# Products of the identity ahead of the first transposes, two groups of transposes later, and half of the last row on ScalarE

## The chip, the cores and the metric

The kernel runs on one NeuronCore of a Trainium2 chip. The core has a matrix engine (TensorE, PE in the profile, with its weight loads listed apart as PEld), VectorE (DVE), ScalarE (ACT), GpSimd (POOL) and SyncE (SP, which here only issues DMAs). Each engine runs its own instructions in the order of the program and waits for the others on semaphores. The metric is the device time of one execution in microseconds; the median of several runs is quoted. Everything is float32.

## The reference

One transformer layer on x of 2 x 1024 x 512: causal linear attention with a residual, then a feed-forward part with 2:4 sparsity and a residual. Cut to what matters:

```python
def reference(x, Wq, Wk, Wv, Wo, w_gate, w_up, w_down):
    x = x + layernorm(attn(layernorm(x)))
    x = x + layernorm(ffn(layernorm(x)))
    return x

def attn(x):                       # 16 q heads, 4 k/v heads, head size 128
    q, k, v = x @ Wq.T, x @ Wk.T, x @ Wv.T          # split into heads
    q, k = rope(q), rope(k)
    qf, kf = elu(q) + 1, elu(k) + 1                 # k, v repeated for 4 q heads
    # over the positions s, with running sums:
    state += k_s[:, None] * v_s[None, :]
    z += k_s
    out_s = (q_s @ state) / (q_s @ z + 1e-6)
    return out @ Wo.T

def ffn(x):
    h = silu(x @ w_gate) * (x @ w_up)
    h = keep_2_largest_of_4(h)                      # by absolute value
    return h @ w_down
```

## The kernel before

**Stages.** The attention goes in 16 steps n: two passes over 8 chunks of 128 positions, each pass with half of the heads. The feed-forward part follows in 4 blocks m of 512 rows. Each projection is done as seven products in place of eight (a Strassen-Winograd scheme): `chain` (its products are numbered 1 to 7 and run in the order 1, 2, 6, 5, 7, 4, 3) multiplies sums and differences of the blocks of x by sums and differences of the blocks of the weight. `FACTORS` says which: product 1 takes blocks (weight 0, x 0), 2 takes (1, 1), 6 takes (3, 4), 5 takes (6, 3). Weight factors 3 to 6 of the first pass are summed by GpSimd (`pooled_sums`, line 604; for wq, lines 2336 and 2339, with lines 2346 and 2350 on VectorE); x factors 3 to 6 are differences by VectorE in `step_input` (lines 967 and 971).

**Start.** Two halves of x are loaded and normalized on VectorE (`step_normalize`, line 300). `step_input(0, 0)` and `step_input(0, 1)` transpose them on TensorE (`transposed`, line 651, four 128x128 transposes against an identity matrix `ident` that GpSimd writes first), ScalarE copies the results out of PSUM (lines 958 and 964), and the first products of `kv_products` and `q_products` (line 1004) begin.

**One attention step n.** The loop at the end of the main function interleaves on TensorE: products of k and v (`kvp`) and of q (`qpr`) for step n + 1, products with Wo (`opr`) for step n - 1, and for step n itself four groups i of heads: `scores(n, i)` (q by k), which VectorE masks into `am` (line 1216), then `attend(n, i)`, which multiplies `am` by v and q by the running state. `outputs(i)` is `attend(n, i)` followed by `scores(n, i + 1)`. The state is carried by VectorE (`state_sums`, lines 1234 and 1240) or copied by ScalarE in a first chunk (line 1248). `attend` also writes the products for the next state, and VectorE and ScalarE divide its result (lines 1347 to 1355).

**q before scores.** Each group of q is turned into features (`features`: VectorE lines 1030 and 1040, GpSimd 1049, ScalarE 1052 and 1054, VectorE 1057), and must then be transposed. Most groups take VectorE's 32x32 transposes and a way through DRAM (`moved`, line 879 and DMAs at lines 886 and 894). The groups in `BY_PE`, all four of step 0 and (1, 1), are transposed by TensorE in `q_transposed`, with a ScalarE copy behind (line 1129).

**PSUM.** Products and transposes use banks of three kinds: "a" (one bank, `ca`), "b" and "e" (two each, `cb` and `ce`). `scores` has one bank (`sc`) and `attend` one two-bank tile (`nm`, pool `ps_nm`). A bank is written again when its readers are done. TensorE transposes take kind "a" unless told otherwise; so does product 2 of each chain.

**Order.** The order on TensorE is the program's own, written out by hand in the main loop. The order on all other engines is computed at build time: `Plan` simulates the layer with assumed lengths (the numbers in `yield "dve", 0.45`), in up to 16 rounds, derives a latest start for every operation from the round before, and keeps the order of the round in which TensorE ends first. So a change of the program's text is followed by a new computation of the order on VectorE, ScalarE, GpSimd and SP for the whole layer. `plan.signal` and `plan.need` name the events that it orders by, and `next_part` releases pieces of the weight preparation that GpSimd does beside the first steps (line 591).

**End.** The last feed-forward block writes its rows as they come; `last_row(y, 1)` handles the last 128 rows: statistics (lines 2184 to 2192), then for each half of 256 columns a normalization (line 300) and the addition of the residual (line 2205) on VectorE and a store (line 2207) by SP for the first and by ACT's queue for the second.

Of the kernel before, what the change touches and what calls it, by code (L numbers as in the profile page):

```python
# [11 lines left out]
F32 = mybir.dt.float32  # L12
BF16 = mybir.dt.bfloat16
AF = mybir.ActivationFunctionType
ALU = mybir.AluOpType
PSUM = bass.MemoryType.PSUM

P = 128
B, S, DM = 2, 1024, 512
# [200 lines left out]
def layer(  # L220
# [17 lines left out]
    nc = tc.nc  # L238

    const = ctx.enter_context(tc.tile_pool(name="const", bufs=1))  # L240
    small = ctx.enter_context(tc.tile_pool(name="small", bufs=3))
# [4 lines left out]
    ident = const.tile([P, P], F32, name="ident")  # L246
    if not isinstance(nc, Blank):
# [8 lines left out]
        fill=0.0,  # L256
# [42 lines left out]
    def normalize(dst, src, mean, rs):  # L299
        nc.vector.tensor_scalar(dst, src, mean, rs, ALU.subtract, ALU.mult)  # L300
# [124 lines left out]
    def left(name, bufs, **more):  # L425
        return actx.enter_context(
            tc.tile_pool(name=name, bufs=bufs, reuse_waits="tile", **more)
        )
# [14 lines left out]
    ps_nm = left("ps_nm", 1, space=PSUM)  # L443
# [503 lines left out]
    def step_input(n, b, kind):  # L947

        if b == 0:
            xf[n] = ln.tile([P, 7, 2, P], F32, tag="xf", name="xf")  # L950
        t = xf[n]
        pt, name = transposed(
            xt[n][:, b, :].rearrange("p (c d) -> p c d", c=NIC), kind, ("xn", n, b)
        )

        def first():
            yield "act", 0.65, 0
            nc.scalar.copy(t[:, 0:2].rearrange("p q k d -> p (q k) d"), pt)
            plan.signal(name)
            plan.signal(("xf0", n))  # L960

        def second():
            yield "act", 0.4, 0
            nc.scalar.copy(t[:, 2], pt[:, 2:4, :])
            yield "xf0", n
            yield "dve", 0.45, 0
            nc.vector.tensor_tensor(t[:, 3], pt[:, 0:2, :], t[:, 0], ALU.subtract)
            plan.signal(name)
            for to, i0, i1 in ((4, 2, 3), (5, 4, 0), (6, 1, 4)):
                yield "dve", 0.45, 0  # L970
                nc.vector.tensor_tensor(t[:, to], t[:, i0], t[:, i1], ALU.subtract)
            plan.signal(("xf", n))
            yield "sp", 0.44, 2
            nc.sync.dma_start(out=xf_dram[n], in_=t)
            yield plan.transfer(896)
            plan.signal(("xf stored", n))

        plan.spawn((first, second)[b]())
# [590 lines left out]
    def run(g, times):  # L1569
        for _ in range(times):  # L1570
            next(g, None)
# [605 lines left out]
    def last_row(y, row):  # L2177
        m, yt = NM - 1, y[:, 2 + row, :]
        yield "y row", row, "a"
        yield "dve", 0.45, 2  # L2180
        st = layernorm_stats(yt[:, 256:512], f"l{row}")
        yield "y row", row, "b"
        yield "dve", 0.45
        nc.vector.bn_stats(st[:, 1, :], yt[:, 0:256])
        mv = small.tile([P, nc.vector.BN_AGGR_DIM], F32, tag=f"mvl{row}", name="mv")
        yield "dve", 0.2
        nc.vector.bn_aggr(mv, st)
        rs = small.tile([P, 1], F32, tag=f"rsl{row}", name="rs")
        yield "act", 0.3
        nc.scalar.activation(rs, mv[:, 1:2], AF.Sqrt, bias=eps)  # L2190
        yield "dve", 0.2
        nc.vector.reciprocal(rs, rs)
        if row == 0:
            yield from write_output(m, 2, (mv[:, 0:1], rs), "dve")
            return
        yn, _ = yield from take("ln", 4, new_yn)
        b, c = place(m, 3)
        yield "residual", m, 3
        xr, _ = res.pop((m, 3))
        for k, queue in enumerate((nc.sync, nc.scalar)):  # L2200
            half_ = slice(256 * k, 256 * k + 256)
            yield "dve", 0.3
            normalize(yn[:, half_], yt[:, half_], mv[:, 0:1], rs)
            yield "dve", 0.42
            nc.vector.tensor_tensor(yn[:, half_], xr[:, half_], yn[:, half_], ALU.add)  # L2205
            yield ("sp", "act")[k], 0.44
            queue.dma_start(out=out[b, c * P : (c + 1) * P, half_], in_=yn[:, half_])
# [119 lines left out]
    with tc.manual_schedule(engines={E.PE, E.Pool, E.SP, E.DVE, E.Activation}):  # L2327
# [51 lines left out]
        plan.spawn(step_normalize(1, None, 0))  # L2379
        plan.spawn(prepare_all())  # L2380
        plan.need(("xn", 0, 1))
        step_input(0, 0, "a")
        step_input(0, 1, "e")
        kvp, qpr = kv_products(0), q_products(0)
        run(kvp, 5)
        run(qpr, 2)
# [7 lines left out]
        for n in range(STEPS):  # L2394
            more = n + 1 < STEPS

            def next_part():
                nonlocal part
                plan.signal(("part", part))
                part += 1  # L2400

            def outputs(i, n=n):
                if n not in (NC - 2, NC):
                    next_part()
                attend(n, i)
                if i < 3:
                    scores(n, i + 1)
                elif 1 < n < STEPS - 1:
                    scores(n + 1, 0)

            if 0 < n < NC - 2:
                next_part()
            if n + 3 < NC:
                plan.spawn(load(n + 3, "x"))
            if n + 2 < STEPS:
                if n + 2 < NC:
                    plan.spawn(step_normalize(n + 2, ("root", n)))
                else:
                    plan.spawn(step_input_again(n + 2))
            if n + 2 == NC:  # L2420
                plan.spawn(load_pass(1, "wq", 2, 512, q_quarter, wq_dram, ("q", n + 1)))
                plan.spawn(load_pass(0, "wkv", 2, 256, kv_quarter, wkv_dram, ("k", n + 1)))
            elif n == NC:
                plan.spawn(load_pass(2, "wo", 4, 256, o_quarter, wo_dram, ("o", n - 1)))
            previous, opr = opr, (o_products(n - 1) if n > 0 else None)
            if n > 0:
                plan.spawn(o_sums(n - 1))
            if n > 1:
                run(previous, 2)
            if not more:  # L2430
                break
            kvp, qpr = kv_products(n + 1), q_products(n + 1)
            run(qpr, 1)
            if n == 2:
                scores(2, 0)
            if n == 0:
                run(qpr, 1)
                run(kvp, 1)
                k_transposed(0, "e")
                q_transposed(0, 0, "e")  # L2440
                run(qpr, 1)
            else:
                run(kvp, 1)
                run(qpr, 1)
                if n == 1:
                    k_transposed(1, "e")
                    first_state(1, 0)
                elif n == NC + 1:
                    first_state(n, 0)
                run(qpr, 1)  # L2450
                if n == 1:
                    scores(1, 0)
                    q_transposed(1, 1)
                    o_transposed(0, 3, "e")
            run(kvp, 1)
            plan.signal(("root", n))
            if n > 0:
                outputs(0)
            else:
                scores(0, 0)  # L2460
            if n + 2 < STEPS:
                plan.spawn(load(n + 2, "rope"))
            run(kvp, 1)
            run(qpr, 1)
            if n == 0:
                q_transposed(0, 1)
                outputs(0)
            run(kvp, 1)
            run(qpr, 1)
            run(kvp, 1)  # L2470
            if n == 0:
                q_transposed(0, 2)
                outputs(1)
                run(kvp, 1)
                run(qpr, 1)
                q_transposed(0, 3)
                run(kvp, 1)
                step_input(2, 0, "a")
                outputs(2)
                step_input(2, 1, "a")  # L2480
                run(qpr, 1)
                outputs(3)
            else:
                outputs(1)
                run(qpr, 1)
                run(kvp, 1)
                run(qpr, 1)
                run(kvp, 1)
                run(opr, 2)
                outputs(2)  # L2490
                if n + 2 < NC:
                    step_input(n + 2, 0, "a")
                run(opr, 2)
            if n + 2 == STEPS:
                plan.need(("prepared",), *(("features", n + 1, i) for i in range(4)))
                rctx.close()
                begin_ffn()
            if n > 0:
                k_transposed(n + 1)
                run(opr, 1)  # L2500
                if n + 2 < NC:
                    step_input(n + 2, 1, "a")
                outputs(3)
# [117 lines left out]
```

## Time and profile before

Three runs: 1264.67, 1262.66 and 1264.32 us, median 1264.32. One execution was profiled.

| | |
|---|---|
| profiled execution, device time | 1261.97 us |
| its span in the profile | 1260.2 us |
| PE busy | 1241.0 us (98%), 6344 instructions |
| PEld busy | 991.6 us (79%) |
| DVE busy | 921.7 us (73%) |
| ACT busy | 478.6 us (38%) |
| POOL busy | 365.7 us (29%) |
| DMA | 266.04 MB, mean 211 GB/s |

The span runs from the first to the last recorded instruction or transfer, and 1.77 us of the device time lie around it. In timelines a row gives start, length, engine, line, operation, tile written and tiles read, shapes and the number of instructions merged; a matmul's length holds its way through the pipeline, so rows overlap, and the distance between starts is the pace. What stands in brackets is the engine's idle time ahead of the row, and what ended it. In the list of waits each row has the engine, its tile and line, then what it waited for, the total, the number of times and the longest. TensorE is nearly always busy, and the idle time of the other engines costs nothing by itself.

### The profile page before, as it was taken

How to read it: one execution, taken by the hardware profiler on the slowest of the kernel's cores; microseconds unless marked ns; L12 is line 12 of the kernel's file. 1: busy time of each engine (PE TensorE's matmuls, PEld its weight loads, DVE VectorE, ACT ScalarE, POOL GpSimd, SP SyncE). 2: the span in 40 equal slices, each digit the busy share in tenths (PEclk: the TensorE clock that was granted, in tenths of full speed). 3: DMA queues.
4: the chain of work that ended last, by engine and by line, in shares of the span. 5: the costliest groups of instructions: out<-in, count | busy, mean ns of one | idle time of the engine just before them, and what ended most of it. 6: DMA issues, size and time to landing. Idle time of an engine off the chain costs nothing. (4 is left out here: it accounts for less than half of the span.)

```text
span 1260.2 us, 18691 instructions
## 1 busy us (share of the span) xinstructions
PE 1241.0 (98%) x6344; PEld 991.6 (79%) x6344; DVE 921.7 (73%) x1751; ACT 478.6 (38%) x941; POOL 365.7 (29%) x319
## 2 busy tenths in 40 slices
PE   7999999999999999999999999999999999999997
PEld 4667776777667776777688888988889988998886
DVE  6898877777656777778764489658993699656873
ACT  3664454443343354445443332133312432133311
POOL 4554443332422455455421105331010101001100
PEclk9999999999999999999999999999999999999999
DMA  7368857678758876676564796589746976677413
GB/s 268 118 223 256 270 185 242 230 229 288 235 190 245 268 231 235 230 227 199 179 193 159 198 269 185 182 237 278 221 126 203 278 214 197 192 232 223 143 50 118
DMA packets 285166, 266.04 MB, mean 211 GB/s; under 512 B 20496, under 2 KB 237072, under 8 KB 282384
## 3 DMA queue, kind: packets, MB, share of 16 engines
q1 hardware_dynamic: 283696, 262.88, 66.9%
q10 hardware_dynamic: 1376, 1.97, 0.5%
q8 instruction: 51, 0.84, 0.3%
q14 instruction: 43, 0.35, 0.1%
HBM read 189.53 MB, written 75.24 MB: 210 GB/s over the span
## 5 line engine op out<-in xcount | busy, mean ns | idle before, releaser
L685 ACT COPY u<-cb 128x512 f32<-128x512 f32 (+1 forms) x234 | 115.7, 496 | 355.3 <-PE cb L1004 117.0
L1355 ACT ACTIVATE o<-nm,den 128x128 f32<-128x128 f32 x256 | 81.5, 367 | 121.2 <-DVE den L1349 79.1
L1049 POOL TENSOR_TENSOR qraw<-qraw,r 128x512 f32<-128x512 f32 x48 | 62.8, 1308 | 214.8 <-DVE qraw L1040 179.6
L1452 PE MATMUL cb<-wo,of 128*128 128x256 f32 x512 | 123.5, 384 | 0.3 <-ACT u L685 0.2
L1004 PE MATMUL cb<-wq,xf 128*128 128x512 f32 x256 | 121.9, 599 | 0.0
L1452 PEld LDWEIGHTS cb<-wo,of 128*128 128x128 f32 x512 | 93.7, 190 | 20.8 <-issue 7.9
L591 POOL TENSOR_TENSOR wraw<-wraw 128x512 f32<-128x512 f32 x68 | 95.5, 1404 | 2.4
L2044 POOL TENSOR_TENSOR h<-h 128x512 f32<-128x512 f32 x16 | 26.8, 1683 | 235.6 <-DVE ht L2033 181.4
L381 PE MATMUL cb<-fxnT,wgu 128*128 128x256 f32 x384 | 87.6, 379 | 0.0
L381 PE MATMUL cb<-fxt,wgu 128*128 128x256 f32 x368 | 84.0, 380 | 0.0
L1004 PEld LDWEIGHTS cb<-wq,xf 128*128 128x128 f32 x256 | 47.2, 190 | 44.7 <-issue 42.8
L381 PEld LDWEIGHTS cb<-fxnT,wgu 128*128 128x128 f32 x384 | 72.7, 190 | 9.8
L381 PEld LDWEIGHTS cb<-fxt,wgu 128*128 128x128 f32 x368 | 69.5, 190 | 10.0 <-ACT u L685 0.8
L1004 PEld LDWEIGHTS cb<-wkv,xf 128*128 128x128 f32 x256 | 47.9, 192 | 31.6 <-issue 25.6
L698 DVE TENSOR_TENSOR y<-u,ce 128x256 f32<-128x256 f32 (+1 forms) x42 | 18.8, 449 | 72.4 <-ACT u L685 57.4
L1004 PE MATMUL cb<-wkv,xf 128*128 128x256 f32 x256 | 68.2, 389 | 0.0
L1452 PE MATMUL ce<-wo,of 128*128 128x256 f32 x256 | 60.5, 379 | 0.0
L2157 POOL TENSOR_TENSOR fyn<-res,fyn 128x512 f32<-128x512 f32 x12 | 15.3, 1275 | 154.8 <-issue 96.0
L1004 PE MATMUL ce<-wq,xf 128*128 128x512 f32 x128 | 60.1, 592 | 0.0
L1057 DVE SCALAR_TENSOR_TENSOR qraw<-qraw,r 128x512 f32<-128x512 f32 x48 | 42.6, 887 | 21.9 <-ACT r L1054 21.7
L2061 PE MATMUL cb<-wd,h 128*128 128x256 f32 x256 | 57.3, 379 | 0.0
L1987 ACT ACTIVATE s<-h 128x1024 f32<-128x1024 f32 x32 | 32.7, 1053 | 64.6 <-DVE h L1983 64.6
(225 smaller groups left out, 2767.2 us busy)
## 6 DMA issues: line engine op xcount, KB each, us to landing
wgu<-us SPq DMA_DIRECT2D x63, 256.0 KB, 4.3
qb<-blocks SPq DMA_DIRECT2D x59, 256.0 KB, 2.3
qT<-qb SPq DMA_DIRECT2D x236, 64.0 KB, 2.7
ob<-blocks SPq DMA_DIRECT2D x58, 256.0 KB, 3.0
of<-ob SPq DMA_DIRECT2D x232, 64.0 KB, 2.6
xf<-xf SPq DMA_DIRECT2D x16, 896.0 KB, 5.1
wd<-in_w_down_dram SPq DMA_DIRECT2D x24, 512.0 KB, 5.7
wd<-d_dram SPq DMA_DIRECT2D x24, 512.0 KB, 5.1
```

The costliest lines, as they stand in the source:

```text
L381: nc.tensor.matmul(bank[:, j, :].rearrange("p (w t) -> p w t", t=32), w[:, k, j, :], xf[xi][:, k], start=(start and j == 0 and k == 0), st ...
L591: nc.gpsimd.tensor_tensor(to, i0, i1, op)
L685: nc.scalar.copy(kept[i], b)
L698: nc.vector.tensor_tensor(dst[:, rows], kept[i][:, rows], b, ALU.add)
L1004: nc.tensor.matmul(bank.rearrange("p h d -> p (h d)"), xf[n][:, xi, k, :], w[wi][:, k, :], start=(start and k == 0), stop=(k == 1), skip_g ...
L1049: nc.gpsimd.tensor_tensor(u, u, r, ALU.add)
L1057: nc.vector.scalar_tensor_tensor(f, u, 0.0, r, ALU.max, ALU.add)
L1355: nc.scalar.activation(t[:, u, :], nmv[:, u // 2, u % 2, 0:HD], AF.Copy, scale=den[:, u // 2, u % 2 : u % 2 + 1],)
L1452: nc.tensor.matmul(bank.rearrange("p h d -> p (h d)"), of[n, xi][:, k, :], weights[gp][2][wi][:, k, :], start=(start and k == 0), stop=(k ...
L1987: nc.scalar.activation(a[:, k::2, :], h[:, k::2, :], AF.Abs)
L2044: nc.gpsimd.tensor_tensor(b12, b22, b12, ALU.subtract)
L2061: nc.tensor.matmul(b[:, j if row is None else 0, :], hts_or_h(m, jb, hi)[:, k, j * P : (j + 1) * P], w[jb][:, k, :], start=(start and part ...
```

## The change

Three things in the order on TensorE, and one in the last row:

- Before the first two `step_input` calls, 18 products of the identity with itself are issued into a new `nm` tile that nobody reads, and two more after these calls. The plan is not told of them.
- In step n = 1, `q_transposed(1, 1)` moves from before `o_transposed(0, 3)` to behind `attend(1, 0)`; one k/v product stands between it and `scores(1, 1)`, which followed `attend(1, 0)` directly before.
- In step n = 0, the two `step_input(2, ...)` calls move behind `outputs(2)` and behind the q product that follows.
- In `last_row`, the second half is normalized by ScalarE as scale * y + shift, with a shift of -mean * scale made by VectorE first; the first half and both additions stay on VectorE.

```diff
@@ last_row
         xr, _ = res.pop((m, 3))
+        shift = small.tile([P, B], F32, tag="shift", name="shift")[:, 0:1]
+        yield "dve", 0.15
+        nc.vector.scalar_tensor_tensor(shift, mv[:, 0:1], -1.0, rs, ALU.mult, ALU.mult)
+        halves = [slice(256 * k, 256 * k + 256) for k in range(2)]
+        yield "act", 0.4
+        nc.scalar.activation(
+            yn[:, halves[1]], yt[:, halves[1]], AF.Identity, bias=shift, scale=rs
+        )
+        yield "dve", 0.4
+        normalize(yn[:, halves[0]], yt[:, halves[0]], mv[:, 0:1], rs)
         for k, queue in enumerate((nc.sync, nc.scalar)):
-            half_ = slice(256 * k, 256 * k + 256)
-            yield "dve", 0.3
-            normalize(yn[:, half_], yt[:, half_], mv[:, 0:1], rs)
+            half_ = halves[k]
             yield "dve", 0.42
             nc.vector.tensor_tensor(yn[:, half_], xr[:, half_], yn[:, half_], ALU.add)
@@ main
         plan.need(("xn", 0, 1))
+        fill = ps_nm.tile([P, 2, 512], F32, tag="nm", name="fill")
+
+        def filler(count):
+            for _ in range(count):
+                nc.tensor.matmul(fill[:, 0, 0:P], ident, ident, start=True, stop=True)
+
+        filler(18)
         step_input(0, 0, "a")
         step_input(0, 1, "e")
+        filler(2)
         kvp, qpr = kv_products(0), q_products(0)
@@ main, in the loop over n
                 if n == 1:
                     scores(1, 0)
-                    q_transposed(1, 1)
                     o_transposed(0, 3, "e")
             run(kvp, 1)
             plan.signal(("root", n))
-            if n > 0:
+            if n > 1:
                 outputs(0)
+            elif n == 1:
+                next_part()
+                attend(1, 0)
+                q_transposed(1, 1)
             else:
                 scores(0, 0)
             if n + 2 < STEPS:
                 plan.spawn(load(n + 2, "rope"))
             run(kvp, 1)
+            if n == 1:
+                scores(1, 1)
             run(qpr, 1)
@@ main, n == 0
                 q_transposed(0, 3)
                 run(kvp, 1)
+                outputs(2)
                 step_input(2, 0, "a")
-                outputs(2)
+                run(qpr, 1)
                 step_input(2, 1, "a")
-                run(qpr, 1)
                 outputs(3)
```

## The prediction

> **What bounds the kernel now.** I read the busy shares first: TensorE (PE) is busy 1241.0 of 1260.2 us, so only its idle time (19.2 us) and slow stretches can be won. The waits of PE, longest first, say where the idle time is.
>
> ```profile
> engine line waited for: us in total, times, longest us
> PE ca L651 <- DVE x L300: 7.6, 1, 7.6
> PE ca L651 <- DVE qraw L1057: 1.6, 1, 1.6
> PE cb L1859 <- DMA wgi<-gs: 0.8, 1, 0.8
> PE ca L381 <- DMA wgu<-in_w_gate_dram: 0.6, 1, 0.6
> PE ca L651 <- ACT qT L1129: 0.5, 1, 0.5
> ...
> PE ca L1004 <- ACT qT L1129: 0.2, 1, 0.2
> ```
>
> The first is the wait for the first normalized x. The 1.6, 0.5 and 0.2 lie at 69.25, 53.75 and 70.55 us, in the stages that the change reorders; the 0.8 and 0.6 lie after 700 us and are not touched. The last matmul ends at about 1253.6, so the tail is another 6.6 us. Next, the timeline of PE at the start.
>
> ```profile
> 7.62 1.09 PE L651 MATMUL ca<-ident,x 128*128 128x128 f32 x4 [7.62 <-DVE x L300]
> 8.49 1.06 PE L651 MATMUL ce<-ident,x 128*128 128x128 f32 x4
> 9.38 2.08 PE L1004 MATMUL cb<-wkv,xf 128*128 128x256 f32 x4
> 11.25 1.40 PE L1004 MATMUL ca<-wkv,xf 128*128 128x256 f32 x4
> 12.48 1.03 PE L1004 MATMUL cb<-wkv,xf 128*128 128x256 f32 x4
> ...
> 25.82 0.60 PE L651 MATMUL ce<-ident,x 128*128 128x128 f32 x4
> ```
>
> Four transposes take 1.06 here and 0.60 later; four products of 256 columns are 1.87 apart (9.38 to 11.25) and later 0.86 (12.48 to 13.34). So PE works at half rate from 7.62 to about 12.0, 4.4 us, although the granted clock of that stretch reads 1.00: here only the durations show it. Last, how full the engines are by stage (columns: stretch, length, then busy time and instructions of PE, PEld, DVE, ACT, POOL).
>
> ```profile
> 55.40:67.00 11.60, 11.49 (x46) 6.10 (x44) 11.46 (x19) 7.64 (x20) 7.40 (x7) 1.00 0.82 264
> 67.00:71.50 4.50, 2.70 (x17) 1.92 (x17) 4.46 (x9) 1.66 (x3) 0.95 (x1) 1.00 0.87 292
> 71.50:80.00 8.50, 8.50 (x45) 5.66 (x44) 7.69 (x19) 4.72 (x10) 3.35 (x3) 1.00 0.72 251
> ```
>
> From 55.4 to 71.5 VectorE (DVE) is busy 15.92 of 16.1 us: there it sets the pace, and the reader should doubt that PE can simply run ahead.
>
> **Part 1, products of the identity.** Added: 18 products and, after the transposes, 2. The identity is written by 1.51 us, so they begin at about 1.6. The nearest row is a 128x128 product at full rate, 0.112 apart (four L1859 products from 800.38 to 800.83); at half rate 0.22, so 18 take 4.0 us and end near 5.6, hidden in the 7.6 us wait. They write the nm bank, whose first other use is at 41.38: nothing waits for them. If all 20 were slow, the last two cost 2 x 0.22 = 0.44 on the path.
>
> What a full rate wins, on PE alone: the ca group ends 0.60 after 7.62, at 8.22; the ScalarE (ACT) copy L958 (0.59, now 8.74 to 9.33) ends at 8.84; the first k/v product starts at 8.89 in place of 9.38; two groups of 0.86 later, at 10.61, the third (factor 6) could start, which now starts at 12.48: 1.87 us. But that product reads a weight sum from POOL and an x difference from DVE.
>
> ```profile
> 9.79 1.26 POOL L604 TENSOR_TENSOR wkv<-wkv,wkv 128x512 f32<-128x512 f32 x1
> 10.46 0.88 DVE L971 TENSOR_TENSOR xf<-xf 128x256 f32<-128x256 f32 x1
> 12.42 1.45 POOL L604 TENSOR_TENSOR wkv<-wkv,wkv 128x512 f32<-128x512 f32 x1
> 12.67 1.48 DVE L971 TENSOR_TENSOR xf<-xf 128x256 f32<-128x256 f32 x1
> ```
>
> POOL's sum ends at 11.05 whatever PE does (its own wait was for the weights' DMA), and the DVE difference, 0.42 long elsewhere (L967), ends at 11.34, 0.29 after POOL; the last one ends 14.15, 0.28 after POOL's 13.87. So each waits for POOL's, and factor 6 starts at about 11.5: 12.48 - 11.5 = 1.0. Of the 1.87, 0.9 turns into a new wait of PE. I take 1.0; the bounds are -0.4 (clock not raised) and 1.4 (POOL's 11.05 alone). What follows (q products, their sums on POOL to 18.79 for a product at 20.23) leaves 1.4 us of room, so the gain travels on.
>
> The Trainium skill, "SBUF — State Buffer", section "SBUF: two separate sides", says that a VectorE operation with two SBUF inputs and a GpSimd one that reads SBUF exclude each other for the whole instruction, and the first to start wins. The difference would now be ready at about 9.70, before POOL's 9.79; by the rule POOL's sum would then end at 11.4, and the gain would be 1.0 again.
>
> By the rows the half rate lasted 4.4 us from the first product, and the 18 products last 4.0, then PE idles about 2 us: that speaks against the filler. The Trainium skill, "TensorE: Matmul & The Clock Gate", Part 1, puts the rise at about 3.4 us of activity in a free-running window, and the fall at an idle window of the same length; by it the clock would rise between 5.0 and 8.4 us and survive the gap, and a late rise would cost up to half of the gain.
>
> **Part 2, the third step's x transposes later (n = 0).** Same instructions. Now PE has finished a product at 53.09 and stands to 53.75 (0.66) because L651 needs the ca bank, freed by the qT copy (ends 53.70); attend(0, 3) starts at 58.65 in place of 58.38 (0.27). Put behind outputs(2), the transposes find the bank free, and attend(0, 2) moves up; it needs the nm bank, freed by the state copy L1248, 53.57 to 53.87 on an ACT that is busy 2.60 of 2.60 us in 50.5 to 53.1. If ACT keeps its order, attend starts 0.3 earlier; if the x normalization (L939, 0.80, at 50.36) goes back, all 0.93 comes. I take 0.6, bounds 0.2 and 0.95. The second x transpose comes later by some 1 us, and its differences (three L971, 63.09 to 66.82) feed the q product at 65.12: a loss here goes to the second rival.
>
> **Part 3, the second step's q transposes later (n = 1).** PE's gaps between scores(1, 0) (ends 67.61) and 74.92 are 1.64, 0.41, 0.11 and 0.11, 2.27 in all. In the new order o_transposed, one k/v product (0.86) and attend(1, 0) (1.85) go ahead of q_transposed. Queued behind attend on PE is all else, and it waits for am and the state sums. Before L1057's qraw (ends 69.07) nothing on DVE changes; add mid 0.25, am 0.41, state 0.27 and kraw<-u,ca 0.41, which frees the ca bank for q_transposed: 69.07 + 1.34 = 70.41. PE reaches q_transposed at 67.61 + 0.43 + 0.86 + 1.85 = 70.75. So DVE just keeps up, with L1057 on u (0.68) and two stream transposes (0.71, 0.69) put off; the q DMAs behind the first of them (a qb store at 70.47, four reads on SP from 72.82, 2.7 to land) can slip by the 2.1 us of these three operations, since scores(1, 2), which reads them, stands at 81.93. The moved x transposes bring one DMA, the xf store (L974, at 66.88), read again only in the second pass. With parts 1 and 2 PE comes up to 1.6 earlier, of which DVE can follow the 1.0 of part 1; some 0.4 to 0.7 is lost. I take 1.6, bounds 0.5 (am stays at 70.96) and 2.2.
>
> **Part 4, the last row.** Now rs (ends 1255.41), normalize 0.41, add 0.43, normalize 0.41, add 0.42, issue at 1257.19. Removed: one DVE normalize (it spaces the next by 0.44). Added: a 128x1 shift, 0.15 with 0.05 to start it (L932), and an ACT half, about 0.45 (copies of 128x256 take 0.37, L939 of 128x512 0.80), beside DVE's half. 0.44 - 0.20 = 0.24. I take 0.2, bounds -0.8 (an ACT table load, 1.28 as at 1247.35, in the path) and 0.25. That Sqrt is followed by a scaled Copy with no load (43.48, 43.69) speaks against the load.
>
> **Sum.** 1.0 + 0.6 + 1.6 + 0.2 = 3.4 us. The profiled execution took 1261.97 (span 1260.2 and 1.77 around it), so 1258.6 for one like it; the median of the three runs, 1264.32, lies 2.35 higher, and 1264.32 - 3.4 = 1260.9.
>
> **Rivals.** The build computes the order of DVE, ACT, POOL and SP anew for the whole kernel, so every stage's order may move; the rivals live there and in the clock.
> First, the clock is not up at 7.6: part 1 gives 0 to -0.4, the rest 2.4: 1264.32 - 2.2 = 1262.1. For: 4.0 against 4.4 us. Against: the transposes add 0.9 to it.
> Second, DVE takes the gain: PE meets it at the q product at 65.12 or at attend(1, 0), and parts 2 and 3 give their lower 0.2 and 0.5, with part 1 halved: 0.2 + 0.5 + 0.5 + 0.2 = 1.4, 1262.9. For: 15.92 of 16.1. Against: DVE's work there is the same, and 0.8 us of it is free by 80.
> Third, slower: the one 0.32 wait of the ca bank for DVE's y (L698), at 135.83, in n = 2, comes back in each of the 14 steps under the new order: 14 x 0.32 = 4.5, less 3.4: 1265.4. It decides from 11 steps on. For: DVE is busy 9.37 of 10 us in 130 to 140. Against: from 140 to 400 PE waits for nothing at all.
> Fourth, the reordering has no effect since the transposes were never last: against it, the 1.6 stands on the very instruction that moves. It would give 1.2, 1263.1, and I count it with the second.
>
> **Chances.** The forecast 0.60 (own range 1259.3 to 1261.8), clock 0.13, DVE 0.15, slower order 0.12. A run of this kernel tells about 0.2% (2.5 us) from no change, so faster means below 1261.8, slower above 1266.8. Faster: 0.60 and a little of the clock rival, 0.62. Slower: the worse half of the third, 0.08. Same: 0.30. The best bounds add to 1.4 + 0.95 + 2.2 + 0.25 = 4.8, 1259.5, and 0.5 for the spread of the runs shown makes the low end 1259.0; the high end, 1264.3, takes in the clock and DVE rivals and leaves the third out.
>
> **What would show it.** Right: in the profile after, transposes of 0.60 at 7.6 and a k/v group 0.86 apart, with PE standing about 0.9 before factor 6 near 11.5; no L651 wait for qraw near 69; the q product that now starts at 74.92 at about 71.7 (74.92 less 3.2); the last issue at about 0.2 less after rs. Wrong: groups of 1.87 at the start; a new PE wait for xf (L971) or am (L1216) between 60 and 72; a table load ahead of the ACT half; waits of 0.3 in many later steps.

## The result and the profile after

The changed kernel takes 1264.41 us (median of 22 runs, 1262.19 to 1268.02), the kernel before, run beside it, 1262.56 (22 runs, 1261.44 to 1265.22, the three already known among them): a ratio of 1.0017, 95% interval [1.0009, 1.0024]. It is slower by 1.85 us where a gain of 3.4 was forecast. The profiled execution took 1262.19 us (span 1260.5), the fastest of its 22, so the traces of before and after differ by less than the medians do.

TensorE's waits in the changed kernel:

```profile
PE fill L2394 <- POOL ident masks.py:199: 1.6, 1, 1.6
PE ca L651 <- ACT kT L1111: 0.9, 1, 0.9
PE ca L651 <- DVE kraw L698: 0.9, 1, 0.9
PE cb L1859 <- DMA wgi<-gs: 0.8, 1, 0.8
PE ce L1452 <- DVE y L698: 0.7, 1, 0.7
PE cb L1452 <- ACT u L685: 0.7, 2, 0.5
PE ce L651 <- DVE kf L1057: 0.6, 1, 0.6
```

The 1.6 us wait for `qraw` is gone. In its place stand two, for `kf` at 63.5 and for `kraw` at 70.2 (0.6 and 0.9), and a third that is new, 0.9 at 98.6, behind the copy of the transposed keys. (Those for `y` and `u`, at 312 and 468 us, come and go between traces of one kernel: e8, the kernel before once more, waits 0.8 for `u`.) The start, from its timeline:

```profile
1.56 6.95 PE L2394 MATMUL fill<-ident 128*128 128x128 f32 x36 [1.56 <-POOL ident masks.py:199]
8.35 0.60 PE L651 MATMUL ca<-ident,x 128*128 128x128 f32 x4
8.79 0.60 PE L651 MATMUL ce<-ident,x 128*128 128x128 f32 x4
9.22 0.61 PE L2394 MATMUL fill<-ident 128*128 128x128 f32 x4
9.67 1.09 PE L1004 MATMUL cb<-wkv,xf 128*128 128x256 f32 x4
10.19 4.09 POOL L604 TENSOR_TENSOR wkv<-wkv,wkv 128x512 f32<-128x512 f32 x3
10.34 4.22 DVE L971 TENSOR_TENSOR xf<-xf 128x256 f32<-128x256 f32 x3
10.59 1.03 PE L1004 MATMUL ca<-wkv,xf 128*128 128x256 f32 x4
11.88 1.10 PE L1004 MATMUL cb<-wkv,xf 128*128 128x256 f32 x4 [0.26 <-DVE xf L971]
```

The clock is up: transposes of 0.60 instead of 1.09, products 0.92 apart instead of 1.87. But the 18 products of the identity are 36 records, last until 8.5 and hold the transposes back to 8.35, where they began at 7.62 before; 0.26 of that is x, whose statistics begin at 4.66 instead of 4.40. The third product of `wkv`, which the prediction put at 11.5, starts at 11.88 (12.48 before).

Engines by stretch, in the columns of the prediction's table:

```profile
55.40:67.00 11.60, 10.96 (x46) 5.68 (x44) 11.50 (x18) 7.48 (x19) 7.22 (x6) 1.00 0.92 294
67.00:71.50 4.50, 3.59 (x32) 3.13 (x31) 4.46 (x8) 1.89 (x4) 3.23 (x3) 1.00 0.68 277
71.50:80.00 8.50, 8.50 (x44) 5.49 (x44) 7.19 (x20) 6.66 (x14) 2.54 (x2) 1.00 0.56 198
```

DVE is still busy 15.96 of 16.1 us from 55.4 to 71.5; PE gained 0.89 us of work in the second stretch (2.70 to 3.59) and lost 0.53 in the first (11.49 to 10.96). The end:

```profile
1256.19 0.15 DVE L2192 RECIPROCAL rs<-rs 128x1 f32<-128x1 f32 x1
1256.38 0.16 DVE L2202 SCALAR_TENSOR_TENSOR shift<-mv,rs 128x1 f32<-128x1 f32 x1
1256.46 0.41 DVE L300 TENSOR_SCALAR fyn<-y,mv,rs 128x256 f32<-128x256 f32 x1
1256.62 0.60 ACT L2205 ACTIVATE fyn<-y,shift,rs 128x256 f32<-128x256 f32 x1 [0.58 <-DVE shift L2202]
1256.91 0.77 DVE L2213 TENSOR_TENSOR fyn<-fx,fyn 128x256 f32<-128x256 f32 x2
1257.71 0.36 ACTq L2215 DMA_DIRECT2D out_dram<-fyn  x1
```

From the end of `rs` (1256.34) to the last issue it now takes 1.37 us, 1.78 before; there is no table load.

### The profile page after: what moved, and what is told of

Its sections match the earlier page's. It is cut to its first block, busy times and chain, and to the rows that moved or that the text cites. A ratio compares the mean times of both kernels' runs of the same rounds, so it can differ in the third digit from the quotient of the medians.

```text
span 1260.5 us, 18755 instructions
## 1 busy us (share of the span) xinstructions
PE 1247.0 (99%) x6384; PEld 997.1 (79%) x6384; DVE 924.1 (73%) x1751; ACT 480.2 (38%) x942; POOL 366.0 (29%) x319
## 4 chain that ended last, share of the span: by engine, by line
PE 86%; DVE 6%; DMA 4%; ACT 1%; issue 1%; SPq 1%; POOL 0%; DVEq 0%; ACTq 0%; POOLq 0%
PE cb L381 14%; PE cb L1004 11%; PE cb L2061 9%; PE cb L1452 7%; PE ce L381 7%; PE ce L1004 5%; PE ce L2061 4%; PE ce L1452 3%; PE ca L381 3%; PE nm L1317 3%; PE cb L1859 3%; PE ca L1004 3%; PE ca L2061 2%; PE nm L1328 2%; PE sc L1203 2%; PE ca L1452 2%
```

## The experiments

Sixteen runs follow (e4, e8 and e16 are known kernels again), each with one profile and five rounds beside the kernel before. Besides the ratio I compare traces by stage: the same TensorE groups are matched in both traces, and the distance between their starts is followed. The table gives what each stage adds to the profiled execution of before (us; negative is a gain); the stages end where, in the first trace of before, these times are reached.

| kernel | to 13.3 | to 62.4 | to 74.9 | to 112 | to 986 | to 1247 | tail | ratio |
|---|---|---|---|---|---|---|---|---|
| after | -0.52 | -0.90 | -0.22 | +1.26 | +0.90 | +0.41 | -0.68 | 1.0017 |
| e4 after again | -0.02 | -0.92 | +0.18 | +1.27 | +0.10 | +1.39 | -0.68 | 1.0016 |
| e1 filler alone | +0.31 | 0 | 0 | 0 | +0.60 | +0.96 | 0 | 1.0012 |
| e7 filler of 8 | +0.55 | 0 | +1.62 | 0 | +1.75 | +0.66 | 0 | 1.0003 |
| e9 wide filler | -0.37 | 0 | 0 | 0 | +3.95 | 0 | 0 | 1.0001 |
| e2 no filler | -0.30 | -0.90 | -0.22 | +1.25 | +0.35 | 0 | -0.67 | 0.9997 |
| e13 after, wide | +0.15 | -0.90 | -0.21 | +1.26 | +2.70 | 0 | -0.66 | 1.0002 |
| e12 no filler, bank e | +1.01 | -0.91 | -0.21 | +0.40 | +0.94 | 0 | -0.67 | 0.9994 |
| e10 x later, last row | +0.57 | +0.33 | -1.25 | 0 | +3.83 | 0 | -0.75 | 0.9990 |
| e11 q later, last row | -0.33 | +0.87 | -2.06 | +1.04 | +6.21 | 0 | -0.65 | 1.0011 |
| e16 before once more | +0.65 | 0 | 0 | 0 | +3.23 | +3.88 | 0 | 1.0008 |
| e8 before again | +0.86 | 0 | +1.62 | 0 | +0.63 | 0 | 0 | 0.9989 |
| e3 old due times | +0.02 | +0.14 | +2.94 | +0.10 | +1.72 | 0 | -0.65 | 1.0023 |
| e5 qT reads first | +0.56 | -0.31 | -0.62 | +1.27 | +1.71 | 0 | -0.74 | 1.0012 |
| e6 e5, bank e | -0.02 | -0.32 | -0.83 | +1.26 | +1.52 | 0 | -0.75 | 0.9998 |
| e14 e13, bank e | -0.06 | -0.91 | -0.23 | +0.40 | +2.50 | 0 | -0.68 | 0.9996 |
| e15 e10, wide | +0.03 | +0.33 | -1.05 | 0 | +2.72 | 0 | -0.75 | 0.9990 |

The column "to 986" varies by several us between traces of one kernel (0, 0.6 and 3.2 for before), so only what repeats is used; the column "to 1247" is 0 in twelve of these rows, and what it holds in the three rows with 18 and 2 products (after, e4, e1) is the first finding. In e16 it is the delayed end of one store at 1017 us (line 300 waited 3.5 us for it) and a fall of the clock behind it; in e7 0.50 of the 0.66 lie at the same place, where line 300 waited 1.4 us for the store.

### The kernel before against itself

e8 and e16 are the kernel before; e4 is the changed kernel once more.

> The kernel before, for a second profile of it: how far the landing of wv (7.89 in the first), the wait at scores(1, 0) and the waits for gi at 988 and 1131 vary without any change. If the landing of wv and the waits at 988 and 1131 vary as much here as with filler, neither is the filler's doing.

> The kernel before against itself beside these three: a ratio within 0.0010 of 1; its runs with a mean granted clock of 0.997 some 1.5 to 1.9 us above those with 0.999, if the fall of the clock at 67 to 72 us makes them.

> The changed kernel once more, for a second profile beside the same runs of before. The 22 times of after lie in two heaps, near 1263.8 and near 1266.4. Theory A: the second heap is the filler running at half rate to its end (36 x 0.22 = 7.9 us, so first transposes near 9.5), and a profile of that heap shows it. Theory B: the start is alike in all runs, and the heaps differ in waits further on.

In e8 and e16 the first weight sum on GpSimd, which waits for Wv, starts at 8.25 and 8.43 us instead of 7.97, and neither has a wait for `gi` near 988 or 1131. The trace of e4 is of a run of 1263.26, so it shows the lower heap once more, and no trace shows the upper one. Against itself the kernel before gave 0.9989 [0.9981, 0.9998] and 1.0008 [0.9997, 1.0019]. So a difference of 0.1% can't be told here, whatever its interval says. The changed kernel's 1.0017 came again as 1.0016 [1.0005, 1.0028] and lies outside.

The profiled run of e8 took 1265.06. In it the granted clock, whose changes the trace records, fell to half at 71.84 us for 3.41 us. The same stretch in the trace of before, then in e8:

```profile
70.55 1.13 PE L1004 MATMUL ca<-wkv,xf 128*128 128x256 f32 x4 [0.24 <-ACT qT L1129]
71.52 0.61 PE L1317 MATMUL nm<-state,qT 128*128 128x129 f32 x4
71.96 0.61 PE L1317 MATMUL nm<-mid,qT 128*128 128x129 f32 x4
```

```profile
71.43 1.71 PE L1004 MATMUL ca<-wkv,xf 128*128 128x256 f32 x4 [0.24 <-ACT qT L1129]
72.93 1.06 PE L1317 MATMUL nm<-state,qT 128*128 128x129 f32 x4
73.79 1.06 PE L1317 MATMUL nm<-mid,qT 128*128 128x129 f32 x4
```

Groups that start 0.44 apart before are 0.86 apart here, and the stage costs 1.62 us. The fall follows the waits at 67 to 71 us. Windows of the clock's own grid, 3.41 us long, with TensorE's busy time in them: the one that ends at the fall in e8, and the one at the same place in the trace of before, after which the clock stayed up:

```profile
68.43:71.84 3.41, 1.60 (x12) 1.00 0.96 333
```

```profile
66.60:70.01 3.41, 1.85 (x13) 1.00 0.86 316
```

Busy for 1.60 us it fell, for 1.85 it did not; where the grid lies differs from run to run. Over the 140 runs of the kernel before that stood beside the experiments, the mean is 1263.23 us at a mean granted clock of 0.999 (87 runs), 1264.28 at 0.998 (43) and 1264.79 at 0.997 (10): up to 1.56 more, as expected. A reading of 0.998 can be a fall (e7) or none (e13), as the clock also falls when TensorE is done, at the end of every trace. The changed kernel read 0.998 in one of its 34 runs and 0.997 in none, so this is not why it is slower.

### The products of the identity

e1 is the kernel before with the 18 and 2 products alone; e2 the changed kernel without them; e7 before with 8 and none behind. The order on the other engines is exactly that of the kernel that each is made from.

```diff
 e1:  +filler(18) ... +filler(2)
 e2:  -filler(18) ... -filler(2)
 e7:  +filler(8)
```

> The kernel before with the 18 + 2 products of the identity alone; the order on every other engine is unchanged. Theory A (the filler overruns the wait it was meant to fill, since each product is two matmuls in the trace, 36 in all and 6.8 us in the profile after, and by an amount that varies): first transposes at 8.3 us or later in place of 7.6, the time between 0.6 us below and 3 us above before, with a wider spread than before. Theory B (the filler does what it should and the loss is all in the new order): 0.6 to 1.0 us below before, spread as before.

> The changed kernel without the products of the identity; its order on VectorE, ScalarE, GpSimd and SP is that of the changed kernel. Theory A: faster than the changed kernel by about what the filler alone costs, 1262 or below where before is 1262.6. Theory B: about 0.6 us slower than the profile of after, and the waits that the profile after shows at 312, 468 and 99 us (0.7, 0.5, 0.9) stand here too, so 1263.5 to 1265.

> The kernel before with 8 products of the identity (16 matmuls, 3.5 us at half rate, done by about 5.1) and none behind the transposes. If the filler costs by overrunning: as before or up to 0.6 us faster. If the start is bound by the weights' DMA and the sums on POOL (wv lands at 7.9 to 9.1, factor 6 starts 3.2 to 3.6 after it), no filler wins more than 0.6, and this one is within 0.5 of before. If the cost is in what the added TensorE instructions move later on (the instruction fetches of TensorE at 985 and 1128 us beside the gate loads): waits for gi near 988 and 1131 come or go with the place of these fetches.

e1: 1.0012 [1.0001, 1.0023]. e2: 0.9997 [0.9986, 1.0007]. e4 and e2 stood beside the same runs of before, with medians of 1265.53 and 1262.33. So the loss comes with the products, not with the moves. In the trace of e1 it is not the overrun of theory A: the transposes start at 7.70 instead of 7.62. e7: 1.0003 [0.9992, 1.0014]. Eight products did not raise the clock (full at 13.31 us; 11.98 in the trace of before); with 18 it is full at 7.19, 6.30 and 5.34 (after, e4, e1). The early clock is real, yet in e1 nothing is won by 13.3 us, and between 986 and 1247 us 0.96 is lost. What TensorE and its weight loads wait for near 988 in e4, then the landing times of the `gi` loads there, in three views of this tile (e4; e13, with the wide filler told of next; before):

```profile
PEld cb L1859 <- DMA wgi<-gi: 0.4, 1, 0.4
PE cb L1859 <- DMA wgi<-gi: 0.2, 1, 0.2
```

```profile
DMA to landing us min/median/max: 4.0/5.4/6.3
```

```profile
DMA to landing us min/median/max: 4.0/4.4/4.9
```

```profile
DMA to landing us min/median/max: 4.5/4.8/5.0
```

The longest takes 6.3 us, 1.3 more than before. The trace has DMA records of kind "instruction": on one queue 51 of 16 KB, about 1 us long, one for some 256 instructions of TensorE, which fits its code. The change adds 80 TensorE instructions (18 + 2 products, two matmuls and two weight loads each), which brings every later fetch forward in the program: from 990.95 and 1130.35 us (before) to 985.32 and 1127.50 (after), 985.22 and 1127.94 (e1), just ahead of the late products at 988 and 1131. The theory: the fetch delays the loads that TensorE is about to need. The landings of one `gi` load near 988 and of one near 1131 fit it in all 18 traces: in after, e1 and e4, where the fetch runs while they are under way, they take 5.80, 6.08 and 6.29 us, and 5.94, 6.19 and 6.42; in the other fifteen, where it does not (in e7 it begins 0.03 us before the second lands), 4.49 to 5.03 and 4.45 to 5.22. In e7, with 32 instructions more, neither wait is there. e9 and e13 fill the same time with a fifth of the instructions, in the kernel before and in the changed one:

```diff
-                nc.tensor.matmul(fill[:, 0, 0:P], ident, ident, start=True, stop=True)
+                nc.tensor.matmul(
+                    fill[:, 0, :].rearrange("p (j d) -> p j d", j=4),
+                    ident,
+                    ident.unsqueeze(1).to_broadcast([P, 4, P]),
+                    start=True, stop=True,
+                )
...
-        filler(18)
+        filler(4)
...
-        filler(2)
```

> The kernel before with 4 products of the identity with four copies of itself (128x512 each) ahead of the first transposes: about as long as the 18 narrow ones (6.1 to 6.9 us by the rows so far), but 16 instructions of TensorE instead of 72 (80 with the two behind). The other engines' order is that of the kernel before. Theory (instruction fetches): the late waits of TensorE for wgi at 988 and 1131, 0.4 to 1.4 us in all four kernels with the filler of 18 and 2 and in no other, come from the added instructions, which move the 16 KB fetch of TensorE's code, one per 256 instructions, from 969 to 985 us; with 16 they move by about 1.4 us, so the waits are gone (below 0.15 us), and the ratio to before is 0.9985 to 1.0003. Rival (the waits follow from the moved start, or from the clock's early rise): the waits stay, 0.4 us and more, and the ratio is 1.0008 to 1.0015. Both expect the full clock at 5 to 7.5 us and the start within 0.5 us of before's.

> The changed kernel with 4 wide products of the identity (16 instructions of TensorE) in place of the 18 and 2 narrow ones (80 instructions); the other engines' order is the changed kernel's. Theory: the changed kernel is slower because its filler's instructions move TensorE's code fetches onto the gate weights' loads at 985 and 1127; without that, waits for wgi at 988 and 1131 below 0.15 us each, and a ratio of 0.9990 to 1.0000 against 1.0017 of the changed kernel. Rival (the new order, or the filler's early clock, makes it slow): 1.0010 to 1.0020 as before.

e9: 1.0001 [0.9992, 1.0009]; e13: 1.0002 [0.9992, 1.0011], 0.0002 above what was expected. The clock is full at 5.19 and 6.01 us, and the loss after 986 us is gone: 0.00 in e9, e13, e14 and e15, all with the wide filler, against 0.41, 0.96 and 1.39 in the three traces with 18 and 2 narrow products. The two pairs, 1.0012 to 1.0001 and 1.0017 to 1.0002, put some 1.4 and 1.9 us on the narrow products; with a kernel straying 0.1% against itself these sizes are rough, and what they hold beyond the late waits is not located. That the added instructions make the late waits is shown; that the fetch itself holds the loads up rests on the landings above, as no run moved the fetch alone.

Why does the start win so little? e13 from 9.5 us on:

```profile
9.54 1.80 DVE L971 TENSOR_TENSOR xf<-xf 128x256 f32<-128x256 f32 x3
9.79 1.03 PE L1004 MATMUL ca<-wkv,xf 128*128 128x256 f32 x4
11.15 2.55 POOL L604 TENSOR_TENSOR wkv<-wkv,wkv 128x512 f32<-128x512 f32 x2
12.53 1.13 PE L1004 MATMUL cb<-wkv,xf 128*128 128x256 f32 x4 [1.71 <-POOL wkv L604]
```

The second product starts 1.46 earlier than before (11.25 to 9.79), and the third 0.05 later, since it waits 1.71 us for POOL's sum. VectorE's differences are ready sooner and start first, and POOL's sum begins only at 11.15, near the end of the third (11.34), and ends at 12.47, where the prediction had 11.05 "whatever PE does". In the changed kernel above it was the other way round: POOL at 10.19, then the differences from 10.34, three in 4.22 us. That agrees with the Trainium skill, "SBUF — State Buffer", "SBUF: two separate sides": one excludes the other, the first to start wins. POOL's first sum, which waits for the DMA of Wv, starts anywhere from 7.97 to 9.13 us over the traces. Over seven traces with the clock up early the third product starts at 12.31 us in the mean (11.88 to 12.69), over ten without any filler at 12.64 (12.05 to 13.03): 0.33 us gained, no more than the spread within either group.

### The two moves

e10 has only the x transposes later, e11 only the q transposes, both with the new last row and without products of the identity.

> The kernel before with the third step's x transposes later (n = 0) and the last row's half on ScalarE; no filler, no move of the second step's q transposes. Theory (the 1.25 us lost between 75 and 112 belong to the move of the q transposes): 1.0 us gained by 62, 0.6 to 0.7 at the end, nothing lost in 75 to 112: 1.6 us, ratio 0.9987, unless the clock falls at 67 to 72, which costs 1.6 us. Rival (any newly planned order gives it back there): 1.0 us gained, 0.8 or more lost in 75 to 112, ratio 0.9995 or above.

> The kernel before with the second step's q transposes later (n = 1) and the last row's half on ScalarE. Theory: 0.2 us gained in 62 to 75, 1.25 lost in 75 to 112 (TensorE waits some 0.9 for the copy of the transposed keys, L1111), 0.65 gained at the end: ratio 1.0003. Rival (the loss comes with the x transposes' order): nothing lost in 75 to 112, ratio 0.9993.

To 62.4 us, where the x transposes lie, after and e2 gain 0.90: TensorE no longer stands before them. The q move alone (e11) gains 2.06 from 62.4 to 74.9; the 0.87 that e11 loses earlier lie at 20 us, where TensorE waits for GpSimd's sums of wq, far from the move. Both moves together gain 1.12 from 13.3 to 74.9 (after and e2; 0.74 to 1.15 in eight traces with both in a newly planned order). They do not add: together they bring TensorE ahead of DVE, which is busy all the time there, and 0.8 is lost at 64.2 with the wait for `kf` and 1.0 more than in e11 at 73.4 with that for `kraw`. Alone, e11 has no wait of TensorE from 60 to 75 us at all.

The 0.92 that e10 gains by 74.9 (0.72 in e15) is not what was expected, 1.0 by 62. By 62.4 it has lost 0.33, as the second transposes wait for a ScalarE copy; then the 1.6 us wait for `qraw` is gone though its transposes did not move, since the newly computed order makes this `qraw` 6 us earlier on VectorE. One line of before, then two of e10:

```profile
68.42 0.68 DVE L1057 SCALAR_TENSOR_TENSOR qraw<-qraw,r 128x512 f32<-128x512 f32 x1
```

```profile
59.15 0.66 PE L651 MATMUL ca<-ident,x 128*128 128x128 f32 x4 [0.57 <-ACT xf L958]
62.21 0.69 DVE L1057 SCALAR_TENSOR_TENSOR qraw<-qraw,r 128x512 f32<-128x512 f32 x1 [0.77 <-ACT r L1054]
```

So a move alone, with an order computed for it, is not a part of the two together. e10: 0.9990 [0.9979, 1.0001]; e11: 1.0011 [1.0002, 1.0020]. Its theory had the loss behind the move, but 0.2 in place of the 2.06; its order loses 1.04 at 97 us, where TensorE waits 0.7 for GpSimd, and, in its profile, 3.7 between 112 and 300.

In 75 to 112 us, e10 loses nothing, and every kernel with both moves in a newly planned order loses 1.25, unless the bank is changed (e12, e14). The place is 98 us. First before, then e2:

```profile
94.02 0.26 DVE L1234 TENSOR_TENSOR mid<-nm,state 128x129 f32<-128x129 f32 x1
94.70 0.81 DVE L1057 SCALAR_TENSOR_TENSOR qraw<-qraw,r 128x512 f32<-128x512 f32 x1
95.03 2.95 POOL L591 TENSOR_TENSOR wraw<-wraw 128x512 f32<-128x512 f32 x2
98.26 0.59 ACT L1111 COPY kT<-ca 128x512 f32<-128x512 f32 x1 [1.52 <-PE ca L651]
```

```profile
94.26 3.28 POOL L591 TENSOR_TENSOR wraw<-wraw 128x512 f32<-128x512 f32 x2
94.66 1.75 DVE L1057 SCALAR_TENSOR_TENSOR qraw<-qraw,r 128x512 f32<-128x512 f32 x1
97.13 0.26 DVE L1234 TENSOR_TENSOR mid<-nm,state 128x129 f32<-128x129 f32 x1
97.42 0.62 ACT L1355 ACTIVATE o<-nm,den 128x128 f32<-128x128 f32 x2 [2.27 <-DVE mid L1234]
98.92 0.59 ACT L1111 COPY kT<-ca 128x512 f32<-128x512 f32 x1
99.56 0.66 PE L651 MATMUL ca<-ident,x 128*128 128x128 f32 x4 [0.93 <-ACT kT L1111]
```

Two things make `mid` late. The new order puts it behind the `qraw` of line 1057, which it stood ahead of; and while DVE's operation started first before, POOL is now 0.40 ahead, and it takes 1.75 instead of 0.81. No run separates the two. ACT waits 2.27 for it with the key copy behind, and TensorE waits for the bank that this copy frees. e12 and e14 give the transposes behind it another bank; e14 has the wide filler too.

```diff
-                    step_input(n + 2, 1, "a")
+                    step_input(n + 2, 1, "e" if n == 1 else "a")
```

> The changed kernel without the filler, with the second half of the fourth step's x transposes (n = 1) in a bank of kind e in place of ca. Theory (what is lost at 98 is the wait for the ca bank that the key copy still holds): the wait of 0.93 us is gone, and 0.6 to 0.9 us of the 1.25 lost in 75 to 112 come back; ratio 0.9991 against 0.9997 of the kernel without this edit. Rival (VectorE, held up by GpSimd's sum at 94.3, is late for all that follows): TensorE waits for something else by 101, the stage still loses 1.0 or more, ratio 0.9997.

> The same with the second half of the fourth step's x transposes in a bank of kind e, so that both losses found are taken away: theory 0.9985 to 0.9995 (the 0.9994 of the kernel without any filler and with this bank, less up to 0.4 us at the start); rival: no better than 0.9997.

The wait is gone, and the stage loses 0.40 instead of 1.25 in both, as the theory had it. Ratios 0.9994 [0.9985, 1.0003] and 0.9996 [0.9986, 1.0005], which can't be told from those without the edit (0.9997, 1.0002). The best found adds the wide filler to e10, with no move of the q transposes:

> The kernel before with the third step's x transposes later, the last row's half on ScalarE and the 4 wide products; the second step's q transposes stay. Theory: 0.4 us at the start, 1.05 by 75, 0.65 at the end, 2.1 us in all, ratio 0.9983 to 0.9990. Rival (the start gains nothing, since the weights' DMA and GpSimd's sums set it): 0.9990 as without the products.

0.9990 [0.9977, 1.0002], as without the filler. With e10 that is twice 0.1% below the kernel before, no more than this kernel strays against itself: neither can be called faster.

### The order on the other engines

e3 makes both moves and the new last row, but the due times by which the other engines' order is computed are taken from the text of before; it has no products of the identity. e5 is e2 with the reads of `of` for group (0, 1) held until those of `qT` for (1, 0) have been issued on SP; e6 is e5 with `q_transposed(1, 1)` in a bank of kind e.

```diff
 e5:  +        if name == ("of", 0, 1):
      +            yield "qT sent", 1, 0
 e6:  -                q_transposed(1, 1)
      +                q_transposed(1, 1, "e")
```

> The reordering of TensorE and the last row's half as in the change, without filler, but VectorE, ScalarE, GpSimd and SP keep the priorities that the build computes for the kernel before; their order differs from before only up to about step 3 and in the last row. Theory B (the loss comes from priorities computed anew in stages that the change does not touch): no waits of PE for y or u at 312 and 468 us, and 1.0 to 2.0 us below before. Rival (the moved transposes themselves cost the time): as slow as the changed kernel without filler.

> The changed kernel without filler, with one dependence more: the four reads of of(0, 1) go to SP only after the four reads of qT(1, 0). Theory C (the new order puts of(0, 1)'s reads and three weight loads ahead of qT(1, 0)'s on SP, so that these are issued at 61.1 to 62.3 us in place of 59.1 and land just when scores(1, 0) needs them, or up to 2 us later, from run to run): qT(1, 0) issued by 59, no run with a wait at scores(1, 0), times in a narrower heap, median 0.5 to 1.5 us below the changed kernel without filler (1262.33), so about 1261 where before is 1262.9. Rival (SP's order does not matter, the waits for kraw, kf and kT take the gain): as the kernel without filler, within 0.4 us.

> As e5, and q_transposed(1, 1) writes a bank of kind e in place of ca, which it shares with the k/v product just ahead. Theory C plus the bank: no wait of PE for kraw (L698) near 70 us (0.9 in the profile after), 0.9 us earlier at 73, and up to 0.9 us less at the end if the wait for kT near 99 does not take it back. Rival (VectorE is the limit there): PE waits for L1057 or at the next step as long.

The reason for e5 is in e4 (waits of TensorE from 60 to 75 us, then SP's issues in time):

```profile
PE sc L1203 <- DMA qT<-qb: 2.2, 1, 2.2
```

```profile
59.86 2.12 SPq L567 DMA_DIRECT2D wraw<-in_wq_dram  x3
62.27 1.75 SPq L894 DMA_DIRECT2D qT<-qb  x4
68.33 0.65 PE L1203 MATMUL sc<-qT,kT 128*64 128x256 f32 x4 [2.17 <-DMA qT<-qb]
```

The new order puts three weight loads and the `of` reads ahead of the four q reads, issued at 59.09 before. In e4 they landed late enough to stop TensorE for 2.2 us; in the first trace of after, issued at 61.06, they did not. The 2.2 took the place of the waits for `kf` and `kraw`, so that e4 is only 0.40 behind after in that stage. With the order mended (reads of `qT` issued at 57.70, no wait at `scores(1, 0)`) e5 gave 1.0012 [1.0004, 1.0021], no better: the plan made anew for this one edit waits 1.0 for `kf` and 0.9 for the key copy. e6, which has these two waits but none for `kraw`: 0.9998 [0.9988, 1.0009]. e3: 1.0023 [1.0012, 1.0033]; it loses only 0.10 from 75 to 112 and has no wait at 312 or 468, but waits 2.0 for the state at 62 to 75, and there the clock falls for 3.41 us (73.47): 2.94 us in that stage. A plan that keeps the old due times does not suit the new text either.

## Why the prediction was wrong

In short: part 1 left out what 80 added instructions move later on, parts 2 and 3 were added up although both draw on the same VectorE, and what the moves still won was lost again at 98 us, in the newly computed order.

**Part 1 (1.0 forecast, a loss of some 1.5 found in e1, and 2.5 between e2 and the changed kernel).** Three steps failed. "The nearest row is a 128x128 product at full rate, 0.112 apart (four L1859 products from 800.38 to 800.83)": these four records are two products, since a float32 product is two matmuls. So 18 products took 6.95, 6.07 and 6.53 us (after, e1, e4), not 4.0, and in the first of these held the transposes back by some 0.5. Next, "POOL's sum ends at 11.05 whatever PE does", and with it "factor 6 starts at about 11.5": the clock did what was hoped, but Wv's landing and the order in which DVE and POOL shut each other out set that sum, which ended at 11.46 to 12.64 in the seven traces with the clock up early, and the product came 0.33 us earlier in the mean. The trace of before had the earliest landing of all (7.97). The third was not in the sum at all: 80 instructions more for TensorE, and with them later landings of the gate weights 980 us on, 0.4 to 1.4 us in the traces. These late waits are the part of the loss that the traces show. The two last products were priced for their own 0.44 us only.

**The rival "clock not up" failed**: the clock was full at 5.3 to 7.2 us. There was no gap of 2 us to survive, as the 18 products lasted until the transposes (at most 0.1 us of idle time between).

**Part 2 (0.6).** Right in mechanism: 0.90 by 62.4 us, within its bounds and near its best case, with all of the wait at 53.75 gone (after, e2). By 62.4 e10 and e15, with this move alone, lose 0.33, so this too hangs on the order of ScalarE.

**Part 3 (1.6).** Alone 2.06 in the stage of the move, within its bounds. "DVE just keeps up" holds for it alone. The failed step is the sum of parts 2 and 3: 0.6 + 1.6 became 1.12 (0.90, then 0.22), because both take the same slack of DVE; the waits for `kf` and `kraw`, or in e4 one of 2.2 us, give back what the moves win. The second rival had this cause and came nearer: 0.7 for the two. That the q DMAs "can slip" was worked out for those that `scores(1, 2)` reads; the new order delayed those for `scores(1, 0)`, which TensorE awaited for 2.2 us in e4.

**The third rival**, a wait that the newly planned order brings, was right in kind and wrong in place: not 0.32 in each of 14 steps but one place at 98 us, 1.25 us, as much as the moves had won.

**Part 4 (0.2).** Right in mechanism; 0.41 us less from `rs` to the last issue, above the bound of 0.25. The mis-sized term is the shift, priced at 0.20: the next normalization starts 0.12 after `rs` instead of 0.10, so it cost 0.02, and the 0.44 came nearly whole. The tail is 0.65 to 0.75 shorter in all twelve traces with the new row; in after the rest lies behind the last issue (2.76 instead of 3.03 us to the end of the span), which nothing in the prediction covers.

**The sum.** In its one profile the changed kernel gains 0.52 at the start, 1.12 to 74.9 and 0.68 in the tail, and loses 1.26 at 98, 0.90 to 986 and 0.41 behind. In the medians the moves and the last row together give 0.9997 (e2), nothing that can be told from no change, and the narrow products add the rest. The base was off too: the three runs of before had a median of 1264.32, all 22 together 1262.56. What makes single runs of the changed kernel take up to 1268 us stays open: the mean granted clock of the run of 1268.02 is 0.999, which speaks against a fall of the clock; the waits that vary from 112 to 986 us are candidates that no run isolated.

## What to carry to other kernels

Price an added instruction also by what it moves: where loads arrive just in time, instructions added at the start can cost more a millisecond later than they gain, so fill idle time with few long ones. Gains of moves that lean on the same busy engine do not add; work out the pair, not the parts, and where a tool plans the order anew for every text, look in the trace whether a gain lies where the edit is. And run a kernel against itself first: here that alone differs by 0.1%.

## What the runs showed of the hardware

- The clock rose after windows of 3.41 us with 3.11 to 3.41 us of TensorE work, and not after windows with 2.28 to 2.87 (e7, e5, e12, e8). It fell in the middle of the kernel after windows with 1.40 to 1.68 (e3, e16, e7, e8, e10), for 3.41 us, and not after windows with 1.72 (e13), 1.75 (e9) and 1.85 (before). Near the end windows with 1.51 (after) and 1.54 (e10) passed without a fall, so the busy time alone does not decide; rise and fall lie 58.03 us (e7, e8) and 61.44 us (e3) apart, 17 and 18 times 3.413. The Trainium skill, "TensorE: Matmul & The Clock Gate", Part 1, gives this free-running window of about 3.4 us, and the traces agree.
- TensorE's code comes in 16 KB pieces, one for some 256 instructions (51 in before), as DMA transfers beside the data, and loads under way during one landed later: 5.80 to 6.42 us instead of 4.45 to 5.22.
- A DVE operation of 0.81 us took 1.75 when a POOL operation started 0.40 us ahead of it: orders that differ by less than a microsecond can change a wait chain.
